# Pacing the gathers of a graph kernel by two engines instead of one

## The chip, the cores and the metric

The kernel runs on one core of a Trainium2 chip. The metric is the device time of one execution in microseconds. The kernel before took 1951.96 us (median of 17 runs, 1944.27 to 1960.3).

## What is computed

There are 16 graphs ("batches") of 1024 nodes with 64 channels, and a dense 0/1 adjacency matrix for each. The reference normalizes each node's channels, drops some edges by a rank rule, and then, for every node and channel, takes quantiles over the node's kept neighbours:

```
h = relu(layernorm(x))
rem = neigh & (skip > 1) & (rank % skip == skip - 1) & mask   # made symmetric
nd = adjacency without rem
s = sort(where(nd, h, inf))                # over the neighbours of each node
agg = sum of w * (value of s at quantile tau), tau 0.25, 0.5, 0.75, w 0.25, 0.5, 0.25
y = relu((h + agg) @ W1 + b1) @ W2 + b2
out = x + y * mask
```

A node has only some ten neighbours, so the kernel makes lists of neighbours and gathers their rows instead of sorting all nodes.

## The kernel before

The nodes of a batch lie in 8 tiles of 128. Each batch is *prepared* (`prepare`, in the order drop, keep, order, collect), while the pair of batches before it is *aggregated*.

- `load` (from L637) reads the adjacency, ACT makes signs (`sg`, L646), TensorE (PE) transposes, and ACT writes `ne` (L662).
- `drop` (from L701): PE counts ranks, ACT writes `dist` (L721, two a tile), DVE marks the edges to remove (`rem`, L722, one a tile).
- `keep` (from L725): PE combines `ne` and `rem`, ACT writes `kept` (L738, two a tile) and the packed neighbour codes (L744). It needs all eight `rem`.
- `order` (from L747): DVE sorts the nodes by their number of neighbours; the result is a one-hot `perm` (L779, eight pieces). It begins with `num` (L750).
- `collect` (from L784): PE permutes the codes (`codeP`, L805), DVE finds the neighbours' numbers one by one (L819 to L847) and writes the list `idx` (L848).

With the list of a batch, POOL issues *gathers* (L963): each fetches one neighbour's row for the 128 nodes of a tile from a table in HBM. There are 67 a batch, 134 a pair, 1072 in all, plus 52 others (for the nodes with most neighbours, and the last writes of these). A pair's rows go into four buffers by tiles: `g0` (tile 0), `g1` (tiles 1 to 3), `g4` (4 and 5), `g6` (6 and 7).

`aggregate` sorts each buffer by a network of minima and maxima on DVE (L998 to L1005), weights the taken rows (L1012), and PE adds them up (`acc`, L1014). After it come a one-hot matrix on DVE (`at_p`, L1075), the two matrix products and the write of the result. `let_go` (L977) puts a tiny DVE memset (`pause`) after every 0.8 us or so of planned sort work.

Two things set the order of the work. `weave` issues gathers and steps of the preparation between the steps of the aggregation by hand-written costs. Then a planner lays the instructions of all engines into each engine's queue by its own estimates of when each can start. A queue is run in order. The queued gathers come out of `issue` (L935), which also *paces* them. `given` holds the last 12 (`BEHIND`) larger DVE instructions in the order of the program: `rem` (L722), `perm` (L779) and first steps of the sort (L1001). Every fourth gather gets a dependency on the oldest of these:

```
if turn[1] % 4 == 0 and len(given) == BEHIND:
    tc.add_manual_dep(ins.ins, given[0].ins.name, ..., reason="pace of the gathers")
```

The dependency counts for the planner's estimates and becomes a wait on DVE's semaphore in POOL's queue, where no earlier wait covers it.

Of the kernel before, what the change touches and what calls it, by code (L numbers as in the profile page):

```python
# [37 lines left out]
AF = mybir.ActivationFunctionType  # L38
# [8 lines left out]
HALF = 512  # L47
# [27 lines left out]
BIG = 3.0e38  # L75

SPREAD = 160
BEHIND = 12


FIRST = CAPS[0] - 1
# [458 lines left out]
def list_layer(  # L540
# [14 lines left out]
    nc = tc.nc  # L555
# [10 lines left out]
    def ask(b, t):  # L566

        if b < B and (b, t) not in asked:
            asked[b, t] = wk.tile([P, N], F32, name="at", bufs=2)
            nc.sync.dma_start(out=asked[b, t], in_=adj[b, t * P:(t + 1) * P, :])  # L570
# [66 lines left out]
    def load(b, fast=False):  # L637

        ne = wk.tile([P, NT, N], FP8, name="ne", bufs=2)
        neT[b] = ne  # L640
        nbs[b] = [wk.tile([P, NT], F32, name=n) for n in ("bias", "half")]
        for t in range(NT):
            ask(b, t)
            at = asked.pop((b, t))
            sg = wk.tile([P, N], BF16, name="sg")
            nc.scalar.activation(sg, at, AF.Sign)  # L646
            ask(*divmod(b * NT + t + 2, NT))
            for n in range(2):
                tp = psum.tile([P, 4, P], F32, name="tp", tag="mx", bufs=3)
                for s in range(4):  # L650
                    m = 4 * n + s
                    nc.tensor.matmul(  # L652
                        tp[:, s], sg[:, m * P:(m + 1) * P], ident16, start=(s == 0), stop=(s == 3 and t // 4 != n),
                        skip_group_check=True,
                    )
                if t // 4 == n:
                    nc.tensor.matmul(tp[:, t % 4], minus16, ident16, start=False, stop=True, skip_group_check=True)
                to = ne[:, 4 * n:4 * n + 4, t * P:(t + 1) * P]
                if fast:
                    nc.vector.tensor_scalar(to, tp, 0.0, None, OP.max, saturate=False)  # L660
                else:
                    nc.scalar.activation(to, tp, AF.Relu, saturate=False)  # L662
            if fast and t == 3:
                number(b, 0, 4)
            yield 0.1
        if fast:
            number(b, 4, NT)
        else:
            number(b, 0, NT)
        yield 1.4  # L670

    def number(b, lo, hi):

        ne = neT[b]
        bias, half = (k[:, lo:hi] for k in nbs[b])
        for n in range(lo // 4, hi // 4):
            cols = slice(n * HALF, (n + 1) * HALF)

            cp = psum.tile([P, HALF], F32, name="cp", tag="mx", bufs=3)
            for k in range(2):  # L680
                for q in range(4):
                    nc.tensor.matmul(
                        cp[32 * q:32 * q + 32], one[:, 1 - k:33 - k], ne[:, 2 * q + k, cols], start=(k == 0),
                        stop=(k == 1), skip_group_check=True,
                    )
            nc.scalar.copy(cnt[:, cols], cp)
        nb = psum.tile([P, NT], F32, name="nb", tag="misc")
        for t in range(lo, hi):
            nc.tensor.matmul(nb[:, t:t + 1], cnt[:, t * P:(t + 1) * P], ones16[:, 0:1], start=True, stop=True)
        nb = nb[:, lo:hi]  # L690

        sk = wk.tile([P, NT], I32, name="sk")[:, lo:hi]
        nc.vector.tensor_scalar(sk, nb, 1.0, None, OP.add)
        many = wk.tile([P, NT], F32, name="many")[:, lo:hi]
        nc.vector.scalar_tensor_tensor(many, nb, 10.0, mask[:, b, lo:hi], OP.is_gt, OP.mult)
        nc.vector.tensor_scalar(sk, sk, 1, None, OP.logical_shift_right)
        nc.vector.tensor_scalar(bias, sk, -1.5, -2047.0, OP.mult, OP.add)
        nc.vector.tensor_scalar(half, sk, 0.5, 1.0, OP.mult, OP.add)
        nc.vector.tensor_tensor(half, half, many, OP.mult)

    def drop(b):  # L701

        ne = neT[b]
        bias, half = nbs[b]
        rem = wk.tile([P, NT, N], BF16, name="rem", tag="wide", bufs=1)
        rems[b] = rem
        for t in range(NT):
            ts = slice(t * P, (t + 1) * P)
            dist = wk.tile([P, N], F16, name="dist")
            for n in range(2):  # L710
                rk = psum.tile([P, HALF], F32, name="rk", tag="mx", bufs=3)
                nc.tensor.matmul(  # L712
                    rk, cnt[:, ts], blocks[:, 4 * n:4 * n + 4, None].to_broadcast([P, 4, P]), start=True, stop=False,
                    skip_group_check=True,
                )
                for s in range(4):
                    nc.tensor.matmul(  # L717
                        rk[:, s * P:(s + 1) * P], ne[:, 4 * n + s, ts], upper, start=False, stop=(s == 3),
                        skip_group_check=True,
                    )  # L720
                nc.scalar.activation(dist[:, n * HALF:(n + 1) * HALF], rk, AF.Abs, bias=bias[:, t:t + 1])  # L721
            given.append(nc.vector.tensor_scalar(rem[:, t], dist, 1.0, half[:, t:t + 1], OP.add, OP.is_equal))  # L722
            yield 0.5

    def keep(b):  # L725

        ne, rem = neT.pop(b), rems.pop(b)
        for t in range(NT):
            ts = slice(t * P, (t + 1) * P)
            kept = wk.tile([P, NT, P], FP8, name="kept")  # L730
            for n in range(2):
                kp = psum.tile([P, 4, P], F32, name="kp", tag="mx", bufs=3)
                nc.tensor.matmul(kp, plus, ne[:, 4 * n:4 * n + 4, ts], start=True, stop=False)  # L733
                nc.tensor.matmul(kp, minus, rem[:, 4 * n:4 * n + 4, ts], start=False, stop=False)  # L734
                for s in range(4):
                    at = (4 * n + s) * P
                    nc.tensor.matmul(kp[:, s], rem[:, t, at:at + P], minus, start=False, stop=(s == 3))  # L737
                nc.scalar.activation(kept[:, 4 * n:4 * n + 4], kp, AF.Relu, saturate=False)  # L738
            code = psum.tile([P, NT, 17], F32, name="code", tag="code", bufs=2)
            for s in range(NT):  # L740
                nc.tensor.matmul(
                    code[:, s], kept[:, s], octet, start=(s == 0), stop=(s == NT - 1), skip_group_check=True
                )
            nc.scalar.copy(pack[:, t, :KEYS], code.rearrange("p s k -> p (s k)"))  # L744
            yield 0.1
# [183 lines left out]

    queue, given = deque(), deque(maxlen=BEHIND)
    turn = [0, 0]

    def issue(many=None):  # L935

        while queue and (many is None or many > 0):
            ins = queue.popleft()()
            if ins is None:
                continue  # L940
            turn[0] += 1
            turn[1] += 1
            many = None if many is None else many - 1
            if turn[1] % 4 == 0 and len(given) == BEHIND:
                tc.add_manual_dep(
                    ins.ins, given[0].ins.name,
                    mybir.DependencyInfo(mybir.DependencyClass.Sync, mybir.DependencyReason.DATA),
                    reason="pace of the gathers",
                )

    def fetch(m, classes=CLASSES, halves=(0, 1)):

# [241 lines left out]
    def weave(main, total, side, side_total):  # L1194

        done = spent = 0.0
        turn[0] = 0
        for cost in main:
            done += cost / total
            issue(max(0, int(done * SPREAD) - turn[0]))  # L1200
            while side is not None and spent / side_total < done:
                got = next(side, None)
                if got is None:
                    side = None
                else:
                    spent += got
        for _ in side or ():
            pass
        issue()
# [11 lines left out]
    def prepare(b):  # L1221
        yield from both(drop(b), load(b + 1) if b + 1 < B else iter(()), normalize(b))
        yield from keep(b)
        yield from order(b)
        yield from collect(b)
# [25 lines left out]


    ahead = load(0, True)
    for _ in range(4):
        next(ahead)
    late_constants()
    drain(both(ahead, drop(0), normalize(0)), keep(0), order(0), collect(0, ((0, 1), (1, NT))))
    fetch(0, halves=(0,))
    issue()
    drain(load(1), prepare(1))  # L1260
    fetch(0, halves=(1,))
    issue()
# [194 lines left out]
```

## Time and profile before

| What | Value |
|---|---|
| median of 17 runs | 1951.96 us |
| the profiled execution | 1953.37 us |
| its span, first to last instruction | 1951.0 us |
| PE busy | 1093.2 us (56%) |
| DVE busy | 1167.7 us (60%) |
| ACT busy | 907.9 us (47%) |
| POOL busy | 1163.6 us (60%) |
| the gathers L963 | 1072, mean 1031 ns, busy 1105.5 us |
| mean granted clock of TensorE | 0.777 |

Engines: PE is the matrix engine (PEld its weight loads), DVE the vector engine, ACT the scalar engine, POOL the engine that issues the gathers, SP the one that issues the other DMAs. A line such as `DVE g L1001 <- DMA g<-htab,idx: 377.9, 29, 57.4` reads: DVE, before instructions of line 1001 that write `g`, sat idle until a DMA that writes `g` from `htab` and `idx` had landed, 377.9 us in total, 29 times, at most 57.4 us. "issue" is idle time that ends with nothing that the profile shows. Where several semaphores are waited for, the one that came last by the profile is named, and this can be a bystander. No engine is busy for more than 60% of the span, so what counts is who waits for whom.

### The profile page before, as it was taken

The page shows a single profiled execution, that of the slowest core. Times are in us where ns is not written, and L with a number is a line of the kernel's source. Part 1 is how long each engine was busy: PE and PEld are TensorE (multiplying, and loading weights), DVE is VectorE, ACT ScalarE, POOL GpSimd, SP SyncE. Part 2 cuts the span into 40 slices and gives each one's busy share as a digit, 9 for nine tenths or more (in the row PEclk, how much of TensorE's full clock was granted, in tenths as well). Part 3 has the DMA queues.
Part 4 walks back from the last instruction along what each step waited for, and adds up shares of the span by engine and source line. Part 5 has one row for each costly group of instructions (what it writes and reads, how often), then busy time and mean ns, then how long its engine had stood idle before and what let it go on. Part 6 is the DMA issues. An engine that isn't in the chain of part 4 may idle for free.

```text
span 1951.0 us, 25536 instructions
## 1 busy us (share of the span) xinstructions
PE 1093.2 (56%) x8385; PEld 681.5 (35%) x8385; DVE 1167.7 (60%) x3635; ACT 907.9 (47%) x2414; POOL 1163.6 (60%) x1129
## 2 busy tenths in 40 slices
PE   5548145885668087822877286467774662214036
PEld 3335033543345054511545153244442331102033
DVE  3414159635299348932499249968695559407981
ACT  7697147586546274822776265438472410001002
POOL 0472743777757775777567766757577777770000
PEclk9779567888879588866998698778887776557568
DMA  4253203335222332322352233314232111110000
GB/s 138 84 158 86 50 16 108 81 88 144 59 71 63 91 89 60 91 62 59 75 135 63 52 84 91 79 21 119 51 75 40 26 36 37 25 26 22 0 1 14
DMA packets 152592, 130.14 MB, mean 67 GB/s; under 512 B 117570, under 2 KB 118082, under 8 KB 152450
## 3 DMA queue, kind: packets, MB, share of 16 engines
q1 hardware_dynamic: 116482, 91.51, 16.7%
q0 software_dynamic: 35968, 36.90, 10.4%
q8 instruction: 68, 1.11, 0.2%
q14 instruction: 74, 0.61, 0.1%
HBM read 112.78 MB, written 13.81 MB: 65 GB/s over the span
## 4 chain that ended last, share of the span: by engine, by line
PE 28%; DVE 21%; POOL 20%; issue 12%; ACT 10%; DMA 8%; POOLq 0%; DVEq 0%; SPq 0%; ACTq 0%
POOL g L963 20%; DMA g<-htab,idx 6%; PE codeP L805 5%; DVE g L1001 5%; DVE g L1005 5%; PE acc L1014 3%; ACT dist L721 2%; DMA at<-in_adj_dram 2%; PE high L1094 2%; PE kp L733 2%; PE kp L737 2%; PE kp L734 2%; ACT sg L646 2%; DVE gg L1001 1%; DVE found L836 1%
## 5 line engine op out<-in xcount | busy, mean ns | idle before, releaser
L963 POOL DMA_INDIRECT g<-htab,idx x1072 | 1105.5, 1031 | 575.8 <-issue 280.7
L1001 DVE TENSOR_TENSOR g<-g 128x768 f32<-128x768 f32 (+3 forms) x408 | 280.9, 706 | 407.7 <-DMA g<-htab,idx 377.9
L1014 PE MATMUL acc<-g,kf 128*128 128x256 f32 (+2 forms) x448 | 147.3, 482 | 289.7 <-DVE g L1012 264.9
L1005 DVE TENSOR_TENSOR g<-g 128x512 f32<-128x512 f32 (+3 forms) x408 | 280.2, 706 | 9.3 <-PE acc L1051 7.2
L721 ACT ACTIVATE dist<-rk,bias 128x512 f16<-128x512 f32 x256 | 170.7, 703 | 151.0 <-DVE rem L722 73.6
L1014 PEld LDWEIGHTS acc<-g,kf 128*128 128x128 f32 x448 | 95.2, 250 | 322.6 <-DVE g L1012 272.8
L805 PE MATMUL codeP<-pack,perm 128*128 128x332 bf16 x1024 | 185.2, 325 | 7.7 <-DVE pause L980 5.9
L652 PE MATMUL tp<-kb,sg 128*128 128x128 bf16 x1024 | 107.7, 245 | 135.6 <-ACT sg L646 111.0
L738 ACT ACTIVATE kept<-kp 128x512 fp8e4<-128x512 f32 x256 | 149.2, 601 | 69.7 <-PE kp L737 68.0
L712 PE MATMUL rk<-kb,cnt 128*128 128x512 bf16 x256 | 109.1, 426 | 84.5 <-ACT dist L721 72.8
L662 ACT ACTIVATE ne<-tp 128x512 fp8e4<-128x512 f32 x240 | 135.3, 611 | 23.9 <-PE tp L652 17.2
L646 ACT ACTIVATE sg<-at 128x1024 bf16<-128x1024 f32 x128 | 134.0, 1066 | 19.4 <-DMA at<-in_adj_dram 19.1
L652 PEld LDWEIGHTS <-sg 128*128 128x128 bf16 x1024 | 80.8, 111 | 159.0 <-ACT sg L646 122.6
L734 PE MATMUL kp<-rem,kw 128*128 128x512 bf16 x256 | 99.9, 391 | 58.7 <-DVE rem L722 58.7
L717 PEld LDWEIGHTS <-ne 128*128 128x128 fp8e4 x1024 | 87.5, 107 | 125.6 <-issue 101.0
L1026 ACT CAST o<-acc 128x512 bf16<-128x512 f32 x48 | 28.3, 590 | 203.4 <-PE acc L1014 194.8
L805 PEld LDWEIGHTS <-perm 128*128 128x128 bf16 x1024 | 96.2, 103 | 72.4 <-DVE perm L779 12.7
L1189 POOL DMA_INDIRECT out_dram<-gx,gto x4 | 4.6, 1147 | 190.0 <-DMA out_dram<-y 187.3
L737 PEld LDWEIGHTS <-rem 128*128 128x128 bf16 x1024 | 80.6, 99 | 105.3 <-issue 64.3
L717 PE MATMUL rk<-kw,ne 128*128 128x128 fp8e5 x1024 | 113.5, 237 | 0.0
L737 PE MATMUL kp<-kw,rem 128*128 128x128 fp8e5 x1024 | 109.9, 223 | 0.0
L809 ACT CAST st<-codeP 128x4 bf16<-128x4 f32 x128 | 21.2, 165 | 177.1 <-PE codeP L805 177.1
(156 smaller groups left out, 2186.4 us busy)
## 6 DMA issues: line engine op xcount, KB each, us to landing
at<-in_adj_dram SPq DMA_DIRECT2D x128, 512.0 KB
g<-htab,idx POOLq DMA_INDIRECT x1072
xt<-in_x_dram SPq DMA_DIRECT2D x16, 256.0 KB
htab<-xt SPq DMA_DIRECT2D x16, 256.0 KB
gtab<-xt SPq DMA_DIRECT2D x16, 256.0 KB
y<-in_x_dram SPq DMA_DIRECT2D x16, 256.0 KB
out_dram<-y SPq DMA_DIRECT2D x16, 256.0 KB
gg<-g SPq DMA_DIRECT2D x16, 96.0 KB
```

The costliest lines, as they stand in the source:

```text
L646: nc.scalar.activation(sg, at, AF.Sign)
L652: nc.tensor.matmul(tp[:, s], sg[:, m * P:(m + 1) * P], ident16, start=(s == 0), stop=(s == 3 and t // 4 != n), skip_group_check=True,)
L717: nc.tensor.matmul(rk[:, s * P:(s + 1) * P], ne[:, 4 * n + s, ts], upper, start=False, stop=(s == 3), skip_group_check=True,)
L721: nc.scalar.activation(dist[:, n * HALF:(n + 1) * HALF], rk, AF.Abs, bias=bias[:, t:t + 1])
L734: nc.tensor.matmul(kp, minus, rem[:, 4 * n:4 * n + 4, ts], start=False, stop=False)
L737: nc.tensor.matmul(kp[:, s], rem[:, t, at:at + P], minus, start=False, stop=(s == 3))
L738: nc.scalar.activation(kept[:, 4 * n:4 * n + 4], kp, AF.Relu, saturate=False)
L805: nc.tensor.matmul(flat, perm[:, t, k * P:(k + 1) * P], pack[:, t], start=False, stop=(t == NT - 1), skip_group_check=True,)
L963: return nc.gpsimd.indirect_dma_start(out=gathered[m, tiles][:, slot, k - lo, h], out_offset=None, in_=tables[2 * m + h], in_offset=bass.I ...
L1001: given.append(nc.vector.tensor_tensor(at(f, df, n), pa, pb, one))
L1005: nc.vector.tensor_tensor(pa if back else pb, pa, pb, other)
L1014: nc.tensor.matmul(acc, ident32, lines[:, s], start=False, stop=(s == now[-1] and not ends), skip_group_check=True)
```

## The change

Every second gather is paced instead of every fourth: in turn by the tenth last larger instruction of ACT and by that of DVE. For this ACT's `ne` (L662), `dist` (L721) and `kept` (L738) are kept in a second list `copied`, and both lists hold 10 instead of 12. The fourth, eighth, twelfth gather and so on still depend on DVE, on the tenth last instead of the twelfth last; the second, sixth, tenth and so on now depend on ACT.

```diff
-BEHIND = 12
+BEHIND = 10
...
-                    nc.scalar.activation(to, tp, AF.Relu, saturate=False)
+                    copied.append(nc.scalar.activation(to, tp, AF.Relu, saturate=False))
...
-                nc.scalar.activation(dist[:, n * HALF:(n + 1) * HALF], rk, AF.Abs, bias=bias[:, t:t + 1])
+                copied.append(
+                    nc.scalar.activation(dist[:, n * HALF:(n + 1) * HALF], rk, AF.Abs, bias=bias[:, t:t + 1])
+                )
...
-                nc.scalar.activation(kept[:, 4 * n:4 * n + 4], kp, AF.Relu, saturate=False)
+                copied.append(nc.scalar.activation(kept[:, 4 * n:4 * n + 4], kp, AF.Relu, saturate=False))
...
-    queue, given = deque(), deque(maxlen=BEHIND)
+    queue, given, copied = deque(), deque(maxlen=BEHIND), deque(maxlen=BEHIND)
...
-            if turn[1] % 4 == 0 and len(given) == BEHIND:
-                tc.add_manual_dep(
-                    ins.ins, given[0].ins.name,
-                    mybir.DependencyInfo(mybir.DependencyClass.Sync, mybir.DependencyReason.DATA),
-                    reason="pace of the gathers",
-                )
+            for last in (given, copied)[turn[1] // 2 % 2:][:1] if turn[1] % 2 == 0 else ():
+                if len(last) == BEHIND:
+                    tc.add_manual_dep(
+                        ins.ins, last[0].ins.name,
+                        mybir.DependencyInfo(mybir.DependencyClass.Sync, mybir.DependencyReason.DATA),
+                        reason="pace of the gathers",
+                    )
```

## The prediction

> **What bounds it now.** I read the page's chain first, then the list of waits, then the idle time of POOL and DVE in order of time. The page's chain, then waits (microseconds in total, times, longest):
>
> ```profile
> POOL g L963 20%; DMA g<-htab,idx 6%; PE codeP L805 5%; DVE g L1001 5%; DVE g L1005 5%; PE acc L1014 3%; ACT dist L721 2%; DMA at<-in_adj_dram 2%; PE high L1094 2%; PE kp L733 2%; PE kp L737 2%; PE kp L734 2%; ACT sg L646 2%; DVE gg L1001 1%; DVE found L836 1%
> ```
> ```profile
> DVE g L1001 <- DMA g<-htab,idx: 377.9, 29, 57.4
> POOL g L963 <- issue: 280.7, 921, 0.3
> ...
> POOL g L963 <- DVE idx L848: 151.6, 5, 70.0
> ...
> POOL g L963 <- DVE at_p L1075: 39.9, 6, 13.3
> ```
>
> The gathers lead the chain, and the two engines wait for each other: DVE's sorts for rows (377.9 us), POOL for index lists. Between, POOL runs gap-free (921 gaps of 0.3). How hard DVE's wait hits is seen in one window (PE, PEld, DVE, ACT, POOL busy):
>
> ```profile
> 850.00:900.00 50.00, 0.00 (x0) 0.00 (x0) 0.00 (x0) 0.00 (x0) 37.81 (x41) 0.50 0.23 49
> ```
>
> Everything stands but POOL: DVE's queue is in order, its head is a sort, and the work behind it feeds PE and ACT. POOL's own idle time comes once a pair, here at the end of pair 4's lists (start, duration, idle before and releaser):
>
> ```profile
> 964.24 0.94 POOL L963 DMA_INDIRECT g<-htab,idx  x1 [0.30 <-issue]
> 976.15 0.94 POOL L963 DMA_INDIRECT g<-htab,idx  x1 [10.97 <-DVE node L850]
> 983.66 1.07 POOL L963 DMA_INDIRECT g<-htab,idx  x1 [6.57 <-DVE at_p L1075]
> ```
>
> The gather at 964.24 is the last that DVE needs before it may finish the next list; the one at 983.66 is the first that reads this list. (The releaser named is an unordered `at_p`; the list's L848 ended at 983.4.) So the kernel runs in **laps**: list ready, gathers run, the last needed one lands, DVE finishes the next list. I number the gathers 0 to 1121 in POOL's queue. The laps start with gathers 134, 301, 436, 593, 726, 861, 1000, at 317.5, 553.0, 754.1, 983.7, 1179.8, 1398.7 and 1592.6 us: 235.5, 201.1, 229.6, 196.1, 218.9 and 193.9 us. Check of the picture on the third: 156 gathers at 1.356 us (754.1 to 964.2) are 211.5; DVE goes on at 968.1 and has the list at 983.4, 19 more; sum 230.5, measured 229.6. After 1592.6 come 122 gathers up to 1754 and a tail of 197 us.
>
> **The change, part by part.** From the built order of both programs, which has no times. POOL's waits on DVE stay (173, now 172), those on ACT rise from 13 to 58. Of the 268 dependencies more, most are covered by an earlier wait. POOL's queue grows by 51 instructions that only wait; such a one takes 17 ns (median at L963), 1 us in all, 15 if each cost an issue gap of 0.3. I take 1: most stand where POOL is ahead.
>
> What costs is what stands ahead of what. The planner moves DVE's sorts with the gathers' due times:
>
> (a) Before, the second batch's `perm` (L779, 8 pieces) stands ahead of the sorts of tiles 4-5 and 6-7 in DVE's queue, and depends on no gather among the last 30 or so: 10 to 12 gathers run while PE and DVE make the list from it. After, in all six laps, `perm` stands behind a first sort step of tiles 6-7, whose last gather comes only 5 to 7 places before the next list's first in four laps (14 and 24 in the last two). POOL's last 2 or 3 gathers of tiles 4-5 even wait for pieces of `perm`. So most of the way from `perm` to list now falls where POOL has nothing to do: (1.4 + 7.1 + 23) less 6 gathers at 1.31 leave 24 us instead of 17.
>
> (b) In two laps a gather of tiles 1-3 waits for the 7th of 16 `kept` (L738) of a stage that starts after DVE has taken the row gathered just before it.
>
> (c) In the first lap the list of batch 3 is read by gather 179 instead of 191, and a sort step ahead of batch 3's last `rem` needs gather 228 instead of 196.
>
> Durations: pitch of unhindered gathers per lap 1.31, 1.348, 1.356, 1.354, 1.41 (then 1.34) and 1.36; from a gather's end to DVE's start 1.4 us (735.17 plus 0.94 to 737.82, less the wake-up):
>
> ```profile
> 735.17 0.94 POOL L963 DMA_INDIRECT g<-htab,idx  x1 [0.30 <-issue]
> 745.41 0.94 POOL L963 DMA_INDIRECT g<-htab,idx  x1 [9.30 <-DVE g L1001]
> ```
> ```profile
> 737.82 0.69 DVE L1001 TENSOR_TENSOR g<-g 128x512 f32<-128x512 f32 x1 [6.04 <-DMA g<-htab,idx]
> ...
> 753.58 0.27 DVE L848 SCALAR_TENSOR_TENSOR idx<-bit,low 128x104 int32<-128x104 f32 x1
> ```
>
> First step of sort 6-7 to last piece of `perm`: 8 x 0.48 plus 1 to 3 steps of 0.69 and small ones, 5.3 to 7.8 by lap. End of `perm` to list: before 18 to 24 us for first batches, which meet no gather (1304.8 to 1323.1, 614.3 to 638.3), 29 to 43 where DVE waits within. After, that wait is gone, and DVE has 21 to 25.5 us of work there by rows; I take 23, keep 21 and 31. Last `rem` to the 7th `kept`: 696.3 to 707, 10.8; with two sort steps and the `rem` ahead, 13.3 (bounds 7 and 19, the whole stage up to `num`).
>
> The laps after, each from the gather that starts it:
> - 134: POOL reaches 179 at 376 and waits for the list, ready at 395.8; 50 more at 1.31 to 461.5; DVE on at 463; from there the list of batch 4 took 55.4 before (405.3 to 460.7), less 8 for one-hot work now done earlier: 510. Gather 247 waits for it; 40 gathers 52.4, landing 1.4, `perm` 7.1, list 23: 594, against 553: +41 (bounds 27 and 52).
> - 293: 110 gathers 148.3, landing 1.4, (b) 13.3, 15 gathers 20.2, 1.4, 5.7, 23: 213.3, +12.
> - 427: 152 gathers 206.1, 1.4, 7.8, 23: 238.3, +9.
> - 585: 113 gathers 153, 1.4, (b) 13.3, 15 gathers 20.3, 1.4, 5.7, 23: 218.1, +22.
> - 717: 74 gathers 104.3, 1.4; then, as before, POOL waits for the first batch's list, 27.5 (1295.6 to 1323.1); 41 gathers 55, 1.4, 7.1, 23: 219.7, +1.
> - 853: 124 gathers 168.6, 1.4, 5.3, 23: 198.3; but 147 gathers run in this lap, 199.9, and these end last: +6.
>
> From gather 1000 on number, waits and order differ little: 0 (bounds -6 and +6, some sort steps). Sum: +91. The profiled execution took 1953.4 us (its span is 1951.0, 2.4 lie around it), 1.4 above the median of the 17 runs; 1953 + 91 = **2044 us**.
>
> One rule speaks against this. The gathers beside busy DVE are longer: 0.92 us in the window above, 1.04 to 1.11 in the laps; at a pitch of 1.25 alone, 988 gathers would save 94 us. The Trainium skill's "SBUF — State Buffer", section "SBUF: two separate sides", says that while DVE holds the port pair it shares with GpSimd, GpSimd can't write descriptors, and blocks fully. By that rule, spacing gathers by DVE's and ACT's progress could win up to all of it, which would cancel the sum. By the rows it is less: DVE's work stays, and POOL's new idle time lies beside it, which pushes no gather out of it. I put nothing for it, and -47 (half) into the range.
>
> **Rivals.**
> 1. *More is lost* (0.14): the other `kept` and `ne` waits on ACT (at gathers 230, 564, 825, 961) also block, up to a stage of 19 us each; about 12 in four laps: 2044 + 48 = 2092. Against: what they wait for depends on no gather of the 20 before (230 apart).
> 2. *Half is hidden* (0.12): DVE now idles less at the sorts of tiles 1-3 (57.4 at 906), lists come at 18 instead of 23 (-30) and (b) at 7 (-12): 2002, or 1985 with a better pitch.
> 3. *Nothing is lost* (0.06): second batches come to `perm` only after the gathers of 6-7 have landed anyway, so the new place costs nothing: 1953. It decides if `num` (L750) comes later than 207 us into a lap of 152 gathers; before it came at 191.6, after a 57 us standstill, which speaks against.
> 4. *Faster* (0.06), one mechanism: the pitch. Place: the six laps. If it falls below 1.30 and the laps lose nothing, 988 x 0.048 = 47: 1906. From 1.25 on it would outweigh even my sum.
> The forecast has 0.62.
>
> **Numbers.** Likeliest 2044. Range 1975 to 2090: down through rival 2 and the low bounds, up to rival 1; it leaves out 3, 4 and what lies above 2090, some 0.18. About 0.2% (4 us) is what a measurement can tell from no change. Faster 0.07 (rival 4 and a little of 3), same 0.04, slower 0.89.
>
> **What would show it.** Right: POOL's idle time ahead of gathers 293, 427, 585 and 717 grows from 17 us (two gaps) to about 24, ended by the list; gaps of 15 to 20 near gathers 179 and 247; 5 to 12 at 408 and 698 behind ACT `kept`; DVE's longest waits for `g` shrink. Wrong: lap lengths as before, or POOL idle mostly at ACT waits elsewhere, or a pitch under 1.3.

## The result and the profile after

The kernel after takes **2043.36 us** (median of 8 runs, 2039.45 to 2046.23), against 1953.08 (median of 47 runs) for the kernel before: ratio 1.0461, 95% interval 1.0444 to 1.0478. The prediction was 2044, slower. The profiled execution after has a span of 2042.3 us, 91.3 more than before.

The page's chain and the list of waits of the kernel after (microseconds in total, times, longest; the gathers are now L966, the first steps of the sort L1004, `idx` L850, `kept` L740, `perm` L781):

```profile
POOL g L966 21%; DMA g<-htab,idx 8%; PE codeP L807 5%; DVE g L1004 5%; DVE g L1008 5%; PE acc L1017 3%; ACT dist L722 2%; PE high L1097 2%; ACT sg L646 2%; DMA at<-in_adj_dram 2%; PE kp L736 2%; PE kp L735 2%; PE kp L739 2%; DVE gg L1004 2%; PE hp L1110 1%
```
```profile
DVE g L1004 <- DMA g<-htab,idx: 522.1, 32, 50.6
POOL g L966 <- issue: 271.8, 892, 0.3
POOL g L966 <- DVE idx L850: 193.3, 7, 69.3
ACT kept L740 <- PE kp L739: 192.6, 27, 58.7
```

The chain is the same one. What grew are the waits: DVE's for gathered rows by 144 us, POOL's for lists by 42, ACT's ahead of `kept` from 68.0 to 192.6. No engine works more than 5 us longer: DVE is busy for 1171.6 us (1167.7 before), PE for 1097.9 (1093.2), ACT for 910.8 (907.9), POOL for 1161.7 (1163.6), the 1072 gathers have the same mean of 1031 ns, and the time from the start of gather 1000 to the end of the span is 356.9 us against 358.4. The first lap starts at 315.3 us (317.5 before). So the loss lies in the six laps:

| lap from gather (before / after) | before | after | difference | predicted difference |
|---|---|---|---|---|
| 134 / 134 | 235.4 | 269.6 | +34.2 | +41 |
| 301 / 293 | 201.2 | 209.0 | +7.8 | +12 |
| 436 / 427 | 229.5 | 232.9 | +3.4 | +9 |
| 593 / 585 | 196.1 | 216.1 | +20.0 | +22 |
| 726 / 717 | 219.0 | 232.7 | +13.7 | +1 |
| 861 / 853 | 193.9 | 209.8 | +15.9 | +6 |
| sum | 1275.1 | 1370.1 | +95.0 | +91 |

I added up POOL's idle times of over 1.5 us in these laps, gap by gap: 109.8 us before, 205.9 after, **96.1 more**. That is the whole loss. Without them a gather takes 1.346 us before and 1.344 after. So the gathers got no slower; POOL stands for longer. Of the 96.1 us, 29.0 are added ahead of gathers 293, 427, 585 and 717, which start the laps; 36.6 lie at gathers 179, 230 and 246 in the first lap, 16.7 at 408 and 698, and the rest, some 14, in the last two laps.

Where it stands is seen at the end of two laps of the kernel after, in POOL's order of time (start, duration, idle before and releaser):

```profile
560.70 1.20 POOL L966 DMA_INDIRECT g<-htab,idx  x1 [0.30 <-DVE perm L781]
562.20 0.94 POOL L966 DMA_INDIRECT g<-htab,idx  x1 [0.30 <-issue]
584.92 1.07 POOL L966 DMA_INDIRECT g<-htab,idx  x1 [21.78 <-DVE at_p L1078]
```
```profile
1004.09 1.20 POOL L966 DMA_INDIRECT g<-htab,idx  x1 [0.30 <-DVE perm L781]
1005.59 0.94 POOL L966 DMA_INDIRECT g<-htab,idx  x1 [0.30 <-issue]
1026.81 0.94 POOL L966 DMA_INDIRECT g<-htab,idx  x1 [20.28 <-DVE idx L850]
```

Gathers 293 and 585, the first readers of the next list, come after gaps of 21.8 and 20.3 us; with the small gaps just ahead 23.5 and 24.2. Before it was 17.0 and 17.5, in two gaps. DVE's order in the first of these windows, cut to what arrives and what comes of it:

```profile
555.32 0.69 DVE L1004 TENSOR_TENSOR g<-g 128x512 f32<-128x512 f32 x1 [12.17 <-DMA g<-htab,idx]
...
558.01 0.48 DVE L781 TENSOR_SCALAR perm<-iota,place_f 128x1024 bf16<-128x1024 f16 x1
...
584.39 0.26 DVE L850 SCALAR_TENSOR_TENSOR idx<-bit,low 128x104 int32<-128x104 f32 x1
```

DVE stood 12 us at a sort step (128x512, the step of tiles 6-7) whose last row was gather 286; `perm` is queued behind it, and the list is ready 26 us after `perm` starts. Behind gather 286 POOL had six gathers left, 287 to 292.

### The profile page after: what moved, and what is told of

The parts are those of the page before. It is cut to its first block, busy times and chain, and to the rows that moved or that the text cites. A ratio compares the mean times of both kernels' runs of the same rounds, so it can differ in the third digit from the quotient of the medians.

```text
span 2042.3 us, 25598 instructions
## 1 busy us (share of the span) xinstructions
PE 1097.9 (54%) x8385; PEld 682.2 (33%) x8385; DVE 1171.6 (57%) x3635; ACT 910.8 (45%) x2414; POOL 1161.7 (57%) x1129
## 4 chain that ended last, share of the span: by engine, by line
PE 27%; POOL 21%; DVE 20%; issue 13%; DMA 10%; ACT 9%; POOLq 0%; DVEq 0%; SPq 0%; ACTq 0%
POOL g L966 21%; DMA g<-htab,idx 8%; PE codeP L807 5%; DVE g L1004 5%; DVE g L1008 5%; PE acc L1017 3%; ACT dist L722 2%; PE high L1097 2%; ACT sg L646 2%; DMA at<-in_adj_dram 2%; PE kp L736 2%; PE kp L735 2%; PE kp L739 2%; DVE gg L1004 2%; PE hp L1110 1%
## 5 line engine op out<-in xcount | busy, mean ns | idle before, releaser
L966 POOL DMA_INDIRECT g<-htab,idx x1072 | 1105.5, 1031 | 669.3 <-issue 271.8
L1004 DVE TENSOR_TENSOR g<-g 128x768 f32<-128x768 f32 (+3 forms) x408 | 281.4, 707 | 524.3 <-DMA g<-htab,idx 522.1
L1008 DVE TENSOR_TENSOR g<-g 128x768 f32<-128x768 f32 (+3 forms) x408 | 281.4, 706 | 10.4 <-PE acc L1054 7.3
L740 ACT ACTIVATE kept<-kp 128x512 fp8e4<-128x512 f32 x256 | 149.6, 601 | 195.2 <-PE kp L739 192.6
L807 PE MATMUL codeP<-pack,perm 128*128 128x332 bf16 x1024 | 177.2, 316 | 26.9 <-DVE pause L983 25.3
L739 PEld LDWEIGHTS <-rem 128*128 128x128 bf16 x1024 | 81.3, 100 | 232.1 <-issue 192.6
L662 ACT ACTIVATE ne<-tp 128x512 fp8e4<-128x512 f32 x240 | 135.4, 612 | 50.3 <-PE tp L652 44.3
L646 ACT ACTIVATE sg<-at 128x1024 bf16<-128x1024 f32 x128 | 134.3, 1067 | 17.6 <-DMA at<-in_adj_dram 17.5
L807 PEld LDWEIGHTS <-perm 128*128 128x128 bf16 x1024 | 93.8, 100 | 91.9 <-DVE pause L983 32.6
L1078 DVE TENSOR_SCALAR at_p<-iota,node 128x512 bf16<-128x512 f16 x256 | 81.1, 372 | 37.3 <-PE low L1100 37.3
L735 PE MATMUL kp<-ne,kw 128*128 128x512 fp8e4 x256 | 101.8, 398 | 1.1 <-ACT dist L722 0.8
```

The lines of the kernel that those rows point to most:

```text
L740: copied.append(nc.scalar.activation(kept[:, 4 * n:4 * n + 4], kp, AF.Relu, saturate=False))
L807: nc.tensor.matmul(flat, perm[:, t, k * P:(k + 1) * P], pack[:, t], start=False, stop=(t == NT - 1), skip_group_check=True,)
L966: return nc.gpsimd.indirect_dma_start(out=gathered[m, tiles][:, slot, k - lo, h], out_offset=None, in_=tables[2 * m + h], in_offset=bass.I ...
L1004: given.append(nc.vector.tensor_tensor(at(f, df, n), pa, pb, one))
L1008: nc.vector.tensor_tensor(pa if back else pb, pa, pb, other)
```

## A measure for the laps

For each run I looked up the gather on which the second batch's `perm` depends in the built order (through whatever sort step stands ahead of it in DVE's queue), and the next list's first reader. The *way* is the time from the end of the one to the start of the other, the *distance* the number of the second gather less that of the first. POOL can cover the distance with work; what the way has over that is idle time.

| run | gathers | distance | way, us | idle in it, us |
|---|---|---|---|---|
| before | 388 to 436 | 48 | 80.7 | 20.4 |
| before | 546 to 593 | 47 | 77.8 | 17.5 |
| after | 286 to 293 | 7 | 31.2 | 23.5 |
| after | 422 to 427 | 5 | 29.1 | 24.1 |
| after | 578 to 585 | 7 | 31.5 | 24.2 |

Before, the long way (edges removed, `kept`, order, list, with waits for rows inside) was covered by 47 gathers but for 17 to 20 us. After, the last dependence lies much closer to the reader: the way is shorter, the cover shorter still.

## The experiments

My theory was that the built order makes the loss: sort steps ahead of `perm` (a), and ahead of the first lists (c), with a small part from the waits on ACT (b). The rival was that the waits themselves, or the larger number of dependencies, hold POOL up.

The first four kernels ran on a chip on which the kernel before itself took 2468 us, the last two on another where it took 2497; three of the first four were run again beside a kernel before of 1951 to 1954 us (the second text on record). What differs there stands further down.

**1. Only the number: 10 instead of 12 on the kernel before, no dependency on ACT.**

```diff
-BEHIND = 12
+BEHIND = 10
```

> The kernel before with 10 instead of 12 in its one list; still every fourth gather, DVE only. In the built order the second batches keep their 29 to 34 places from perm to the first reader of the list, but the list of batch 4 now depends on gather 262 of 264 (before: 196 of 255), and that of batch 8 on 554 of 556 (before: 434 of 547). Theory 'order': the first lap grows by some 20 us and the fourth by 5 to 10: 1970 to 1985. Rival 'waits': no wait on ACT is added, so 1953.

> The kernel before with 10 instead of 12 in its one list; still every fourth gather, DVE only. Repeated, since in the run before the kernel before itself took 2468 us. Against a kernel before at 1953: theory 'order': the list of batch 4 now depends on gather 262 of 264 (before: 196 of 255), that of batch 8 on 554 of 556 (before: 434 of 547); the first lap grows by some 20 us and the fourth by 5 to 10: 1970 to 1985. Rival 'waits': no wait on ACT is added, so 1953.

Measured: 2508.66 on the first chip, ratio 1.0222 (1.0128 to 1.0315); run again 2062.47, ratio **1.0561** (1.0526 to 1.0596). I had expected little, and it costs more than the whole change. POOL's idle time in its laps is 225.8 us, 116 more than before. POOL, at the start of the lap from gather 436 of this kernel:

```profile
776.67 1.06 POOL L963 DMA_INDIRECT g<-htab,idx  x1 [9.10 <-DVE perm L779]
778.03 1.20 POOL L963 DMA_INDIRECT g<-htab,idx  x1 [0.31 <-DVE perm L779]
786.55 0.94 POOL L963 DMA_INDIRECT g<-htab,idx  x1 [7.32 <-DVE rest L821]
800.36 0.94 POOL L963 DMA_INDIRECT g<-htab,idx  x1 [12.88 <-DVE at_p L1075]
```

That is 29.3 us of idle time, against 20.4 in the same lap before. DVE in the same window:

```profile
742.54 1.32 DVE L1001 TENSOR_TENSOR g<-g 128x768 f32<-128x768 f32 x2 [9.27 <-DMA g<-htab,idx]
...
748.80 0.47 DVE L722 TENSOR_SCALAR rem<-dist,half 128x1024 bf16<-128x1024 f16 x1
...
771.33 0.27 DVE L750 TENSOR_REDUCE num<-pack 128x8 f32<-128x64 bf16 x1 [9.64 <-ACT pack L744]
...
775.10 0.48 DVE L779 TENSOR_SCALAR perm<-iota,place_f 128x1024 bf16<-128x1024 f16 x1
...
799.83 0.26 DVE L848 SCALAR_TENSOR_TENSOR idx<-bit,low 128x104 int32<-128x104 f32 x1
```

The head is a sort step of tiles 1-3 that waits for gather 411; the last `rem` stand behind it, then come `kept`, `num`, `perm` and the list. Before, the step in that place waited for gather 388. The distance fell from 48 to 25 gathers, the way only to 59.4 us. My expectation had looked at the places of `perm` and of the list against the list's reader, and not at how long the way from that gather is when the last `rem` are still to come. The same in the laps up to 593 (distance 34, way 73.2, idle 30.4) and 726 (17, 57.4, 37.5).

**2. The change with 12 instead of 10.** All 58 waits of POOL on ACT stay.

```diff
-BEHIND = 10
+BEHIND = 12
```

> The changed kernel with both lists holding 12 instead of 10; POOL has the same 58 waits on ACT. In the built order the second batch's perm stands behind gather 264, 398, 556, 689, 817 and 951, that is 26 to 49 places before the first gather that reads its list, as in the kernel before (25 to 50) and not as in the changed one (5 to 24). Theory 'order' (the place of perm and of the list behind gathers in DVE's queue sets the laps): 1945 to 1975 us. Rival 'waits' (POOL being held by ACT is what costs): 2025 to 2060, as in the changed kernel.

> The changed kernel with both lists holding 12 instead of 10; POOL has the same 58 waits on ACT. Repeated for the same reason. In the built order the second batch's perm stands 26 to 49 places before the first gather that reads its list, as in the kernel before (25 to 50) and not as in the changed one (5 to 24). Against a kernel before at 1953: theory 'order': 1945 to 1975 us. Rival 'waits': 2025 to 2060.

Measured: 2426.65 on the first chip, ratio 0.9853 (0.9747 to 0.9958); again 1968.33, ratio **1.0081** (1.0061 to 1.01). Idle time in the laps is 125.9 us, 16 more than before. The lap's end in POOL's order shows the gaps of before, 10.2 and 6.6 us:

```profile
966.92 0.94 POOL L966 DMA_INDIRECT g<-htab,idx  x1 [0.30 <-issue]
978.02 0.94 POOL L966 DMA_INDIRECT g<-htab,idx  x1 [10.15 <-DVE node L852]
985.53 1.07 POOL L966 DMA_INDIRECT g<-htab,idx  x1 [6.57 <-DVE at_p L1078]
```

So 58 waits on ACT and every second gather paced cost 0.8% at 12, where the same at 10 cost 4.6%. Distance and way fit this: 29 gathers, 53.0 to 54.2 us, 15.8 to 16.7 idle in three laps. Beside run 1: at 10 the turns with ACT win some 20 us (2062 to 2043), at 12 they lose some 14. The two parts of the change don't add up; each has a built order of its own.

**3. The change without the waits on ACT**: the dependencies on ACT's instructions count for the planner, but no semaphore is waited for.

```diff
-                        mybir.DependencyInfo(mybir.DependencyClass.Sync, mybir.DependencyReason.DATA),
+                        mybir.DependencyInfo(
+                            mybir.DependencyClass.Sync if last is given else mybir.DependencyClass.NoSync,
+                            mybir.DependencyReason.DATA,
+                        ),
```

> The changed kernel with its dependencies on ACT kept for the planner only: the built order is that of the changed kernel within a place, and POOL's waits on ACT fall from 58 to 13. Theory 'order': 2043 less the idle time ahead of gathers 408 and 698 that ACT ended (4.9 and 11.8 us), some 2025, at most 2045. Rival 'waits': back to the kernel before, under 1980.

> The changed kernel with its dependencies on ACT kept for the planner only: the built order is that of the changed kernel within a place, and POOL's waits on ACT fall from 58 to 13. Repeated, since in the run before the kernel before itself took 2468 us. Against a kernel before at 1953: theory 'order' (the place of perm and of the list behind gathers in DVE's queue sets the laps): 2043 less the idle time ahead of gathers 408 and 698 that ACT ended (4.9 and 11.8 us), some 2025, at most 2045. Rival 'waits' (POOL being held by ACT is what costs): under 1980.

Measured: 2514.96 on the first chip, ratio 1.0247 (1.016 to 1.0335); again 2035.83, ratio **1.0431** (1.039 to 1.0472). The median is 7.5 us below the kernel after, but this isn't clear of noise: its four runs took 2028, 2029, 2042 and 2043 us, and the two intervals overlap. So the waits themselves are worth between nothing and some 17 of the 90 us, by the ends of the intervals; the rest is the order in which the instructions were built. The profile is of the run of 2029. At the lap's end POOL stands as in the kernel after:

```profile
1000.01 1.19 POOL L969 DMA_INDIRECT g<-htab,idx  x1 [0.30 <-DVE perm L781]
1001.51 0.94 POOL L969 DMA_INDIRECT g<-htab,idx  x1 [0.30 <-issue]
1023.38 1.16 POOL L969 DMA_INDIRECT g<-htab,idx  x1 [20.93 <-DVE at_p L1081]
```

What went in this profile are the gaps at 408 and 698 (the laps from 293 and 585 are 4.5 and 11.7 us shorter) and the one at 230, for which gaps at 242 and 246 grew: the first lap is only 1 us shorter. In the kernel after they read:

```profile
739.45 0.95 POOL L966 DMA_INDIRECT g<-htab,idx  x1 [0.30 <-issue]
745.30 0.94 POOL L966 DMA_INDIRECT g<-htab,idx  x1 [4.90 <-ACT kept L740]
```
```profile
1179.86 0.94 POOL L966 DMA_INDIRECT g<-htab,idx  x1 [0.30 <-issue]
1192.63 0.94 POOL L966 DMA_INDIRECT g<-htab,idx  x1 [11.82 <-ACT pack L746]
```

The second names `pack`, an ACT instruction beside the `kept` that is waited for.

**4. Every second gather paced by DVE alone, at 10.**

```diff
-            for last in (given, copied)[turn[1] // 2 % 2:][:1] if turn[1] % 2 == 0 else ():
+            for last in (given,) if turn[1] % 2 == 0 else ():
```

> Every second gather paced, by the tenth last larger instruction of DVE alone; no new wait on ACT, waits on DVE rise from 173 to 269. In the built order perm of a second batch stands 27, 22, 7, 19, 25 and 26 places before the list's first reader, and the list of batch 4 depends on gather 259 of 261. Theory 'order': the first lap grows by some 20 us, the third by some 9, the rest by 0 to 6 each: 1980 to 2000. Rival 'waits' (any denser waiting of POOL costs): 2000 to 2045, as POOL gets 96 waits more, twice as many as in the changed kernel.

Measured, on the first chip only: 2519.48, ratio 1.0278 (1.0178 to 1.0378). It lies within the intervals of runs 1 and 3 there, and tells nothing apart.

**5. The change, with the sorts of tiles 4 to 7 queued behind `perm`.** Each of their steps gets a dependency on the last piece of the second batch's `perm`, which counts for DVE's own order only; this is aimed at (a).

```diff
+            pins['perm', b] = ins
...
-    def sort(lines, plan, first, coef, acc, in_turn=False):
+    def sort(lines, plan, first, coef, acc, in_turn=False, pin=None):
+        def behind(ins):
+            if pin is not None:
+                tc.add_manual_dep(
+                    ins.ins, pin.ins.name,
+                    mybir.DependencyInfo(mybir.DependencyClass.NoSync, mybir.DependencyReason.DATA),
+                    ...
+            return ins
...
-                given.append(nc.vector.tensor_tensor(at(f, df, n), pa, pb, one))
+                given.append(behind(nc.vector.tensor_tensor(at(f, df, n), pa, pb, one)))
...
+                    pins.get(('perm', 2 * m + 3)) if lo >= 4 else None,
```

> The changed kernel with one more rule for the planner: each sort step of tiles 4-5 and 6-7 is queued on DVE behind the last piece of the second batch's perm (order only, no wait). In the built order perm then stands 20, 27, 20, 19, 27 and 37 places before the first gather that reads its list (changed kernel: 7, 5, 7, 5, 14, 24); the list still depends on a gather 2 to 6 places before. POOL's 56 waits on ACT stay. Theory 'order': five laps back to about the lengths before, 196 to 235 us each, and the first list of all no later than before: 1940 to 1985. Rival 'waits': 2025 or more. Rival 'first lap' (most of the loss sits in batches 3 and 4, not in perm): 1990 to 2020.

Measured: 2001.92, ratio **1.0242** (1.0211 to 1.0272): 41 of the 90 us come back. 16 of them lie ahead of the first lap, which now starts at 299.2 us; so the rule moves more of the order than it was aimed at. Ahead of the readers of the next lists (292 and 293, 426 and 427, 583 and 584, 716 and 717) POOL now stands for 18.8, 18.0, 19.6 and 19.7 us, against 23.5 to 25.2 in the kernel after and 16.4 to 17.5 before. The third of these, to be held against the 21.8 and 20.3 shown above:

```profile
972.20 0.94 POOL L970 DMA_INDIRECT g<-htab,idx  x1 [0.30 <-issue]
982.51 0.94 POOL L970 DMA_INDIRECT g<-htab,idx  x1 [9.37 <-DVE rest L824]
993.64 0.94 POOL L970 DMA_INDIRECT g<-htab,idx  x1 [10.19 <-ACT dist L722]
```

That is 21 of the 29 us of (a), and about all by which the idle time in the laps falls (from 205.9 to 184.5 us). The laps from 293 and 427 take 200.1 and 229.9, as before the change (201.2, 229.5); in the first of them the gap of 4.9 us at 408 went as well. The first lap (266.8) and the later ones (208.4, 232.5, 205.7) keep most of their loss, so (a) isn't all, and the expectation of a time below 1985 failed. `perm` is early, but in the built order the list's last instruction still depends on a gather 2 to 6 places ahead of its reader.

**6. and 7. The same sorts behind the list itself**, the last `idx` of the second batch, in the kernel after (6) and in the kernel before (7): the edit of 5 with

```diff
+            pins['idx', b] = nc.vector.scalar_tensor_tensor(
...
+                    pins.get(('idx', 2 * m + 3)) if lo >= 4 else None,
```

> The changed kernel with the same rule as the kernel before got here: the sorts of tiles 4-5 and 6-7 behind the second batch's list. In the built order the list depends on a gather 19, 18, 19, 18, 19 and 51 places before its first reader. 18 gathers take 24 us, the way from perm to list 23 and perm 5 to 8: POOL idles some 5 to 8 us a lap instead of 24. Theory 'order': 1880 to 1930, slower than the kernel before with this rule. Rival 'waits': as the changed kernel, 2025 or more.

> The kernel before, with each sort step of tiles 4-5 and 6-7 queued on DVE behind the second batch's finished list. In the built order that list then depends on gather 254, 388, 546, 680, 813 and 984, that is 47, 47, 46, 45, 48 and 14 places before its first reader instead of 2 to 6. Theory 'order' (laps are gathers plus the way from the last needed one to the list): the idle time of POOL ahead of each lap, 17, 17, 17.6, 16.4, 12.4 and 4.8 us, goes, some 80, and part of the 43.8 ahead of gather 134: 1830 to 1880. Rival 'another limit' (the sorts that now come later, or the preparation, end last instead): 1930 to 1960, with POOL's idle time at other waits.

Measured: 6 takes 1966.47, ratio **1.0069** (1.0048 to 1.0089); 7 takes **1890.75**, ratio **0.9667** (0.9634 to 0.97), and beats both kernels, by some 60 and 150 us. Kernel 7 at the start of the lap from 592, DVE and then POOL:

```profile
919.67 0.48 DVE L779 TENSOR_SCALAR perm<-iota,place_f 128x1024 bf16<-128x1024 f16 x1
...
943.38 0.25 DVE L849 SCALAR_TENSOR_TENSOR idx<-bit,low 128x104 int32<-128x104 f32 x1
...
950.48 0.69 DVE L1014 TENSOR_TENSOR g<-g 128x512 f32<-128x512 f32 x1 [2.52 <-DMA g<-htab,idx]
```
```profile
949.14 0.94 POOL L967 DMA_INDIRECT g<-htab,idx  x1 [0.30 <-issue]
950.39 0.95 POOL L967 DMA_INDIRECT g<-htab,idx  x1 [0.30 <-issue]
951.64 1.44 POOL L967 DMA_INDIRECT g<-htab,idx  x1 [0.30 <-issue]
```

The list is ready at 943.6, 7 us before its first reader at 950.4, and POOL runs through. The gaps at 301, 592 and 861 are gone; idle time in the laps is 63.7 us. What is left stands mostly at first batches' lists (10.4 and 18.0 at gathers 165 and 167, 13.4 at 812 to 815), and 6 to 9 us each ahead of 435, 725 and 998. The sum: 46 us less idle time, 18 from an earlier first lap, 7 given back by a pitch of 1.354 instead of 1.346 (864 gathers), and 3 less after the laps.

Kernel 6 has no step of tiles 4 to 7 ahead of its lists either, but a distance of 18 or 19 gathers, where kernel 7 has 46: from 565 to 584 a way of 36.0 us and 11.7 of idle time. This is DVE there, then POOL:

```profile
942.81 0.96 DVE L1017 TENSOR_TENSOR g<-g 128x768 f32<-128x768 f32 x1 [60.96 <-DMA g<-htab,idx]
...
953.11 0.69 DVE L781 TENSOR_SCALAR perm<-iota,place_f 128x1024 bf16<-128x1024 f16 x1
...
977.57 0.26 DVE L851 SCALAR_TENSOR_TENSOR idx<-bit,low 128x104 int32<-128x104 f32 x1
```
```profile
965.44 0.94 POOL L970 DMA_INDIRECT g<-htab,idx  x1 [0.30 <-DVE keys L822]
978.10 1.07 POOL L970 DMA_INDIRECT g<-htab,idx  x1 [11.71 <-DVE at_p L1092]
```

A step of tiles 1-3 (128x768) stands for 61 us at the head of DVE's queue until 942.8, when gather 564 has landed and 565 has just been issued, and `perm` stands behind it. In kernel 7 the step in that place needs gather 546. The 76 us between the two kernels are POOL's idle time in the laps, 139.2 us in kernel 6 and 63.7 in kernel 7. Half of the difference, 38 us, lies ahead of the second batches' lists, where the distances differ (59.5 against 21.9 us); the other half is at first batches' lists and at gather 698, for which distance and way were not taken. Both times are above what I expected, 7 by 11 us, 6 by 36.

**8. and 9. No pace at all**, in the kernel before (8), and with the edit of 7 (9):

```diff
-            if turn[1] % 4 == 0 and len(given) == BEHIND:
+            if turn[1] % 4 == 99 and len(given) == BEHIND:
```

> The kernel before, without any dependency for the pace. In its built order the waits of POOL on DVE fall from 173 to 39, and the lists of the second batches are read by gathers 309, 443, 601, 735, 869 and 1005 and depend on gathers 42 to 43 places earlier (before, 2 to 6 places in five of these laps), their one-hot perm on the same ones (before, 43 to 48 places). Theory of the distance: 42 gathers at 1.36 us are 57 us, against the way from that gather to the list of some 56 to 79 us (rem, kept, order and list, by the laps of the kernel before and of the run with BEHIND 10): 0 to 22 us of idle time a lap, on average less than the 17 of before, so 1840 to 1955, and the lists wait for no late sort. Rival, the pace itself is what keeps DVE supplied: without it POOL goes ahead and then stands at a list or a buffer for 30 us or more a lap: 1990 to 2060.

> The kernel before without any dependency for the pace, and with every sort step of tiles 4 to 7 queued behind the last list instruction of the second batch. The lists of the second batches then depend on gathers 95 to 101 places ahead of their first readers, 129 us and more at 1.36 us. Theory: this covers the whole way from the last needed gather to the list (56 to 79 us), so no idle time is left ahead of the laps, and the rest is 299 (first list) plus 988 gathers at 1.36 (1344) plus the tail after the last lap of 194 to 205: 1837 to 1865. Rival, the waiting only moves: the sorts pushed back free their buffers late, and POOL stands for buffers or first batches' lists by 5 to 15 us a lap, as it did when the same was done to the kernel before with its pace (1891): 1875 to 1940.

Measured, on the chip of 2497 us: 8 takes 2630.18, ratio 1.0509 (1.0422 to 1.0596), 9 takes 2598.61, ratio 1.0404 (1.0343 to 1.0464). Inconclusive: on that chip PE and ACT have long stops of their own, POOL stands for 50 us and more ahead of some lists in both kernels, and experiment 2, slower by 0.8% elsewhere, was faster by 1.5% there. Whether the pace helps at all on an undisturbed chip stays open.

## Why the prediction was right

**The laps** carry it: start of the first lap -2.2 us, laps +95.0, rest -1.5, together the 91.3 of the span. That the loss sits there, as POOL's idle time ahead of lists, is what was predicted. That 2044 was met within 1 us is luck: the single laps were off by -7 to +13 us, and these errors add up to 4.

**(a)** The idle time ahead of 293, 427, 585 and 717 was predicted at 24 and measured at 23.5, 24.1, 24.2 and 25.2. Before, it was 68.0 us in the four laps together; after, 97.0. Run 5, aimed at this, takes 21 of the 29 us back, so the cause is shown for these gaps; they are 30% of the loss, and the laps from 293 and 427 alone come back to their old length. Runs 1 and 6 add that the step ahead of `perm` need not be one of tiles 6-7: one of tiles 1-3 with a late gather does it too.

**(b)** The sum charged 13.3 us and a landing of 1.4 in each of two laps for the stage up to `kept`. In the trace POOL stood for 4.9 and 11.8, which is the 5 to 12 named as the sign, but some 10 and 3 us less than charged. In run 3's profile, without these waits, the two laps are 4.5 and 11.7 shorter.

**(c)** Gaps of 15 to 20 were expected near gathers 179 and 247: 14.3 at 179 and 13.5 at 246, a little less than named. The gap of 8.7 at 230 was in rival 1, not in the forecast: it ends at ACT's `pack`. Rival 1's other three places, 564, 825 and 961, show none. The first lap came 7 us shorter than predicted, since the list read by gather 247 was ready 185 us into the lap (500.5) and not 192 (510). No run undoes (c) alone, so its share is read from the trace.

**The pitch** was put at nothing, and it is nothing: mean gather 1031 ns in both. Against its sum the prediction set the Trainium skill's "SBUF — State Buffer", section "SBUF: two separate sides". By that page the full block comes from DVE operations in a 2-port mode, or from those with two SBUF inputs against a GpSimd operation that reads SBUF; the prediction left this condition out. The traces show a small price instead: from gather 134 on, the gathers during which DVE idles take 0.94 us (330 of them before, 384 after), and those that run beside sort steps for over 90% of their time 1.14 us before and 1.18 after. Spacing the gathers by DVE and ACT bought none of the 94 us. Even run 7, which fills 46 us of POOL's idle time, pays only 0.008 us a gather.

**Mis-sized terms**, which happened to cancel, beside (b):

- 427: 5 us too much, all of it the pitch. I took 1.356 of before for 152 gathers, 206.1 us; they took 201.4, or 1.325 each.
- 717: 13 us too little. I took the wait for the first batch's list as before, 27.5 us; it was 33.8 (DVE goes on at 1349.9, the list ends at 1383.7). From there to the next lap it was 91.9 us for my 86.5.
- 853: 10 us too little. I let the gathers end last, with `perm` behind gather 976 and the list 23 us after it. But a second sort step, between `perm` and the list, waits for gather 992: DVE is at 1666.4 there, the list ends at 1685.1, and gather 1000 waited 10.2 us for it. I had counted the steps ahead of `perm`, not those behind it.

**"DVE's longest waits for `g` shrink"** was half wrong: the longest did (57.4 to 50.6), but their sum rose by 144 us. I took early lists for rows that come earlier; with POOL idle for 96 us more, they come later. Rival 2 rested on this as well.

What the prediction didn't ask is which half of the change does it. That gathers now depend on ACT suggests the waits; 1, 2 and 3 show that the step from 12 to 10 decides, that the waits on ACT are worth some 17 us at most, and that the two interact. Why the planner chooses these orders at 10 and not at 12 was not tried: it follows from its estimates, and no run here opens them.

## What to carry to other kernels

Where two in-order queues feed each other, find for each stage the last outside event that its result depends on, through every instruction queued ahead, and set the way from there against the work that the other queue still has: the difference is the idle time of every round. A dependency that is meant to pace may cost little as a wait and much through the order that a planner builds around it, so read the built order first, and try the number alone, the waits alone and the order alone. Here one explicit rule, no sort of tiles 4 to 7 ahead of the list that fetches the next rows, made the kernel before 3.3% faster, while each change of the pace that was tried beside a kernel before of some 1952 us made it slower.

## What was not expected of the hardware

On two chips the kernel before took 2468 and 2497 us where others take 1951 to 1954, and most single instructions are about as long as elsewhere: in the run without pace there, gathers have a mean of 1032 ns and `dist` 699; the matmuls `tp` have 256 against 245, at a granted clock of 0.695 against 0.777. PE and ACT have stops of up to 74 us that end with nothing that the profile shows. The first row is of the kernel before, on a chip of 1952 us, the second of the run without pace, from the costliest groups of the two pages:

```profile
L721 ACT ACTIVATE dist<-rk,bias 128x512 f16<-128x512 f32 x256 | 170.7, 703 | 151.0 <-DVE rem L722 73.6
```
```profile
L721 ACT ACTIVATE dist<-rk,bias 128x512 f16<-128x512 f32 x256 | 171.0, 699 | 316.3 <-remote 274.0
```

The busy time is the same, the idle time ahead twice as long, and "remote" means that the trace names no instruction or transfer that ended it. Summed over all stops of more than 4 us that end with "remote" or "issue", it is 480 us on PE's matmuls and 978 on ACT, against none on either in the kernel before. Their cause stays open. Ratios from these chips don't carry over here: experiment 2 had 0.985 there and 1.008 elsewhere.
